# Projecting layer 1's first chunk inside layer 0's tail: a two-layer transformer block on one Trainium2 core

## The chip, the core and the metric

The kernel runs on one core of one Trainium2 chip. The core has five engines with a queue of instructions each: TensorE (PE in the profile, with its weight loads as PEld), VectorE (DVE), ScalarE (ACT), GpSimd (POOL) and SyncE (SP), which here only issues transfers. Work meets in SBUF, in eight PSUM banks of 2 KB per partition, and in DRAM, over 16 DMA engines. The metric is the time of one execution in microseconds (us); before the change three runs gave 1144.49, 1149.3 and 1153.21 us, median 1149.3.

## The reference, cut to what matters

The input x is 2 x 1024 tokens of 256 numbers. Each of two layers computes

```python
xn = _layernorm(x)
x = x + attention(xn) + ffn(xn)
```

Layer 0 has causal attention with 32 heads of 8 over 1024 tokens and a gated feed-forward part with FP8 roundings. Layer 1, whose start the change touches, attends between the 16 heads of one and the same token:

```python
q = apply_rope((x @ wq.T).reshape(b, s, 16, 16), inv_freq)   # k the same way
v = (x @ wv.T).reshape(b, s, 16, 16)
scores = einsum('bshd,bstd->bsht', q, k) / sqrt(16)
attn = einsum('bsht,bstd->bshd', softmax(scores), v)
out = attn.reshape(b, s, 256) @ wo.T
```

Its feed-forward part is `silu(gate) * up` with ternary weights, an RMS norm and a second ternary matrix.

## The kernel before, in words

**Tiles.** The 2048 tokens are 16 tiles of 128 (`xs`), and four tiles make a chunk of 512. `xnT[c]` holds the normalised chunk c with the features on the partitions. Layer 1 takes the chunks in the order 0, 1, 3, 2.

**Layer 0** (`attention0`, from line 802) runs over pairs (b, i): a batch b and a tile of 128 queries i, in an order that ends with (1, 2), (1, 1), (1, 0). The work is laid out by hand in slots. Each pass of `one_slot` (line 1311) emits some units of the row maxima for a later tile (`max_unit`, L1010: matmuls into `ps_s`, three PSUM banks, then a reduction on DVE, L1034), a piece of layer 0's feed-forward part, a piece of a "late" layernorm on every third slot, and whatever `after` has made due. Then `weigh` (L1081) emits the scores of two groups of heads into `ps_t` (four banks), their exponentials on ACT (L1096) and, on the diagonal blocks (j == i), a mask on POOL (L1100). Every second slot `gather` (L1114) adds the products with v of the pair of slots before into `acc` (the eighth bank). `normalise`, `turn_rows` and `output` (L1128 to L1161) follow a finished tile; the last instruction of a tile is the addition of the bias to x on POOL (L1160). PE's order is the order of the code (`manual_schedule`); the order on the other engines is chosen by the compiler's scheduler among what is emitted, with `tc.issue_after` as an extra edge. TAIL = 16: the maxima are spread so that they are all emitted when 16 slots of `weigh` are left. Those slots are the last four of (1, 2), the eight of (1, 1) and the four of (1, 0).

**Layer 1** (`layer1`, from line 408) takes its order from a heap of times written out by hand: `at(delay, f)` (L752) puts f at a time, and the loop at L797 emits in order of these times. For the first chunk (p = 0) they are:

- -5.0, -4.1, -3.2, -2.3: `project(0, i)` (L461) for the four tiles: the product with wq and wk (`pqk`, L467), the rotation by two multiplications on DVE (L475) and an addition on POOL (L482), the product with wv (`pv`, L486), and a copy on ACT (L490). Half a unit of time later `turn` (L493) transposes q and k on PE (`pt`, L498), copies them on ACT (L499), sends all six 128 x 128 squares to a DRAM scratch (`qkv<-all`, L501) and loads from it three pieces of 128 KB: q, k and v by heads, into partitions 32i to 32i + 15 of the slots (`qs`, `ks`, `vs`, L503).
- -4.7 to 2.3 in steps of 1: `ffn_unit(0, hc)` (L666), twelve matmuls `f1gu` (L678) into two banks `ps_gu`, with ACT, DVE and POOL work behind it.
- -1.81 and -0.01: `busy_later` (L766), 7 and 10 matmuls whose results nobody reads (L145).
- -0.4: `project(1, 0)` of the second chunk.
- 0.0: `scores(0, 0)` (L516): `sq` (L522) reads the q and k slots of all four tiles; DVE reduces (L530), the maxima go to DRAM (`mscr<-m`, L532) and come back as a row of the q slot (`qs<-mscr`, L535); then `shifted` (L551) computes the scores again (`sk`, L557) and ACT takes the exponential.

Before all of these, `load_same(0)` (L442) puts eight constant pieces (four of 72 KB from 9 rows, four of 64 KB from 8 rows) into the slots, and POOL fills the v slot with ones (L433). Behind the last load of the first chunk, SP issues `load_same(1)` and the load of `wo` (L508 to L510). The slots take over SBUF from layer 0, so the first of these loads waits for layer 0's last addition on POOL.

The line numbers are those of the kernel before. Three functions carry the change: `two_layers`, `layer1` and `attention0`.

## Time and profile before

| what | us |
|---|---|
| three runs | 1144.49, 1149.3, 1153.21 (median 1149.3) |
| the profiled execution's own time | 1146.81 |
| its span, first to last instruction | 1144.6 |
| PE, DVE, ACT, POOL busy | 1006.4, 761.1, 608.3, 399.9 |
| last reduction of the maxima, start | 733.4 |
| layer 0's last addition on POOL, end | 774.2 |
| first `pqk` of layer 1, start | 772.5 |

The profile is one execution of the program. The page gives totals; the trace behind it answers by engine and by time, counted in us from the start of the span. The chain of waits follows the work back from its last instruction: a line has a start, a length and what ran there, and a line "DMA a<-b" is the time in which the chain waited for that transfer. In a table of stretches, (x n) is the number of instructions, PEclk the share of its full clock that TensorE was granted, and DMA the mean share of the 16 DMA engines in use, added up over their packets, so that it can pass 1.

### The profile page before, as it was taken

Reading aid. Unit: us, or ns where it says so; the run is one execution under the profiler, and the core shown is the slowest. Engines: PE = TensorE matmul, PEld = TensorE weight load, DVE = VectorE, ACT = ScalarE, POOL = GpSimd, SP = SyncE. Lnnn points to the kernel's source line nnn. Section 1 sums busy time; section 2 is a strip of 40 time slices with the busy share of each in tenths; the row PEclk is TensorE's granted clock in tenths of the full one; section 3 lists DMA queues with packets and bytes.
Section 4 is the critical chain, followed back from the end, with each engine's and each line's share of the span. In section 5 each row is a group of like instructions: output and inputs, shape, how many; then the busy total and the mean of one; then the engine's idle time right before and its main releaser. Section 6 shows DMA issues by size and latency. Waiting matters only on the chain.

```text
span 1144.6 us, 19966 instructions
## 1 busy us (share of the span) xinstructions
PE 1006.4 (88%) x7676; PEld 484.2 (42%) x7699; DVE 761.1 (66%) x1434; ACT 608.3 (53%) x1097; POOL 399.9 (35%) x440
## 2 busy tenths in 40 slices
PE   5858797897998989998989989988899999899897
PEld 2333331232332323332323333424577677676576
DVE  6567978889687897889886988504554544543521
ACT  3113571674455757678867767853463444434331
POOL 2007224424135121411133254547644535423400
PEclk9758896998899989999999999999899999999989
DMA  5332101101101000100000100006621241343100
GB/s 177 114 104 78 58 1 41 21 21 35 57 7 42 15 28 10 29 18 7 22 15 14 28 15 17 5 1 105 82 48 38 55 83 34 80 75 52 39 20 20
DMA packets 63888, 49.04 MB, mean 43 GB/s; under 512 B 20905, under 2 KB 57257, under 8 KB 63657
## 3 DMA queue, kind: packets, MB, share of 16 engines
q1 hardware_dynamic: 58592, 39.05, 15.2%
q0 software_dynamic: 4112, 8.26, 3.0%
q8 instruction: 60, 0.98, 0.4%
q10 hardware_dynamic: 1088, 0.46, 0.1%
q14 instruction: 36, 0.29, 0.1%
HBM read 34.12 MB, written 15.20 MB: 43 GB/s over the span
## 4 chain that ended last, share of the span: by engine, by line
PE 51%; DVE 27%; DMA 8%; ACT 7%; POOL 3%; issue 3%; SPq 2%; DVEq 0%; ACTq 0%; POOLq 0%
DVE mx L1034 14%; PE acc L1116 8%; PE s L1086 7%; PE sk L557 4%; PE f1gu L678 4%; PE f1o L717 3%; PE m L1022 3%; PE pqk L467 3%; PE sq L522 3%; DMA qscr<-ptq 2%; PE gu L301 2%; DMA qs<-mscr 2%; ACT p L1096 2%; PE m L994 1%; SPq L946 1%
## 5 line engine op out<-in xcount | busy, mean ns | idle before, releaser
L1034 DVE TENSOR_REDUCE mx<-m 128x1 f32<-128x512 f32 (+3 forms) x608 | 373.0, 653 | 100.5 <-PE m L1022 53.8
L1096 ACT ACTIVATE p<-s 128x512 f32<-128x512 f32 x576 | 307.7, 606 | 123.0 <-PE s L1086 119.0
L1116 PE MATMUL acc<-p,v 128*9 128x512 f32 x1152 | 170.1, 610 | 1.8 <-ACT p L1096 1.2
L1100 POOL TENSOR_SCALAR_AFFINE_SELECT p<-p 128x512 f32<-128x512 f32 x128 | 82.9, 672 | 152.5 <-ACT p L1096 152.3
L1022 PE MATMUL m<-k,qmain 64*128 64x512 bf16 (+3 forms) x384 | 95.5, 358 | 44.4 <-DVE mx L1034 34.5
L1022 PE MATMUL m<-kmain,qmain 64*128 64x512 bf16 (+3 forms) x384 | 81.7, 330 | 21.8 <-DVE mx L1034 20.0
L1022 PEld LDWEIGHTS <-qmain 64*128 64x128 bf16 x768 | 50.5, 99 | 81.3 <-issue 52.1
L994 PEld LDWEIGHTS <-ident_h 64*128 64x128 bf16 x832 | 45.7, 97 | 82.6 <-issue 59.7
L994 PE MATMUL m<-mask_q,ident_h 64*128 64x128 bf16 (+3 forms) x832 | 73.9, 221 | 1.9 <-DVE mx L1034 1.7
L1086 PE MATMUL s<-qmain,k 64*128 64x512 bf16 x288 | 65.8, 394 | 6.3 <-DVE att L1139 2.7
L1086 PE MATMUL s<-qmain,kmain 64*128 64x512 bf16 x288 | 65.3, 385 | 6.7 <-ACT p L1096 4.2
L1086 PE MATMUL s<-qlast,k 35*128 35x512 bf16 x288 | 62.8, 391 | 0.0
L1086 PE MATMUL s<-qlast,klast 35*128 35x512 bf16 x288 | 61.5, 381 | 0.0
L1086 PEld LDWEIGHTS <-k 64*128 64x128 bf16 (+1 forms) x576 | 21.0, 95 | 93.0 <-issue 84.5
L678 PEld LDWEIGHTS <-wgu_bf 128*128 128x128 bf16 x384 | 38.3, 101 | 41.5 <-issue 5.0
L557 PE MATMUL sk<-qs,ks 25*128 25x128 f32 x512 | 48.3, 423 | 8.1 <-DMA qs<-mscr 7.9
L687 DVE SCALAR_TENSOR_TENSOR h<-h,f1gu 128x512 f32<-128x512 f32 x32 | 21.9, 686 | 48.8 <-ACT h L686 48.8
L565 ACT ACTIVATE p<-sk 128x2048 f32<-128x2048 f32 x16 | 30.0, 1877 | 44.3 <-PE sk L557 44.3
L692 POOL TENSOR_TENSOR sq<-h 128x512 f32<-128x512 f32 x28 | 29.1, 1039 | 67.2 <-DVE h L688 65.8
L1159 POOL TENSOR_TENSOR x<-x,aos 128x256 f32<-128x256 f32 x16 | 12.6, 789 | 112.7 <-ACT aos L1158 112.7
L530 DVE TENSOR_REDUCE m<-sq 128x16 f32<-128x2048 f32 x16 | 36.6, 2286 | 20.9 <-PE sq L522 19.3
L154 POOL TENSOR_TENSOR hp<-hrest,hp 128x512 bf16<-128x512 f32 x32 | 37.0, 1157 | 31.5 <-ACT hp L153 31.4
(288 smaller groups left out, 1799.0 us busy)
## 6 DMA issues: line engine op xcount, KB each, us to landing
qmain<-qscr SPq DMA_DIRECT2D x64, 96.0 KB
qkv<-all SPq DMA_DIRECT2D x16, 384.0 KB
qscr<-ptq POOLq DMA_DIRECT2D x6, 384.0 KB, 4.1
x<-in_x SPq DMA_DIRECT2D x16, 128.0 KB
qmain<-qscr SPq DMA_DIRECT2D x32, 64.0 KB
qs<-qkv SPq DMA_DIRECT2D x16, 128.0 KB
ks<-qkv SPq DMA_DIRECT2D x16, 128.0 KB
vs<-qkv SPq DMA_DIRECT2D x16, 128.0 KB
```

The lines of the kernel that those rows point to most:

```text
L154: engines[1].tensor_tensor(parts[2], r, parts[1], ALU.subtract)
L467: nc.tensor.matmul(pqk, x[k], wqk[:, k, :], start=(k == 0), stop=(k == 1))
L530: last(nc.vector.tensor_reduce(m, ps, AX.X, ALU.max, negate=True))
L557: nc.tensor.matmul(ps[:, s, r, :], columns(k, slice(S * s, S * s + HD + 9), 4 * b + r), columns(q, slice(S * s, S * s + HD + 9), 4 * b + r ...
L678: nc.tensor.matmul(ps[g], wgu_bf[:, k, g * HID + hc * P : g * HID + (hc + 1) * P], x_parts[n][m][:, k, :], start=(k == 0 and m == 0), stop ...
L994: nc.tensor.matmul(out[e][:, :, lo:], ident_h[rows, t, :], rhs.to_broadcast([HALF, out[e].shape[1], P - lo]), start=start and t == 0, stop ...
L1022: nc.tensor.matmul(sc[e][:, s * width : (s + 1) * width], qst[b, i][0][rows, p, :], kst[b][0][rows, lo // 512, p // 4, 0:width], start=not ...
L1034: reduced = nc.vector.tensor_reduce(mx[b, i][:, part, e, pairs[0] : pairs[0] + n], sc[e][:, : n * width].rearrange("p (s k) -> p s k", s=n ...
L1086: nc.tensor.matmul(sc[e], kst[b][n][rows, j // 4, u, j % 4 * P : (j % 4 + 1) * P], qst[b, i][n][rows, 4 * u : 4 * u + 4, :], start=n == 0, ...
L1096: nc.scalar.activation(p, sc[e], AF.Exp, scale=scale)
L1100: nc.gpsimd.affine_select(out=by_head, in_=by_head, compare_op=ALU.is_ge, fill=0.0, base=0, pattern=[[0, 4], [1, P]], channel_multiplier=-1,)
L1116: nc.tensor.matmul(acc[32 * s : 32 * s + HD0 + 1, :], vst[b][:, j, 4 * G + s, :], ps[s], start=(j == 0), stop=(j == i),)
```

## The change

Three things go out of layer 1: the four calls of `project` for the first chunk, the `turn` that each of them puts into the heap, and the two `busy_later` entries at -1.81 and -0.01. In their place the heap gets, at -5.0, four calls of `to_slots`, which is the old end of `turn`: the twelve loads from the DRAM scratch (and, behind the last, `load_same(1)` and `wo`, as before).

The work itself goes into layer 0. `first_projections` is a generator of eight steps: `rows(0)`, `rows(1)`, `turned(0)`, `rows(2)`, `turned(1)`, `rows(3)`, `turned(2)`, `turned(3)`. `one_slot` takes one step on every even slot once all maxima are emitted; what is left is emitted behind the last `gather`. `rows(i)` does what `project` did, `turned(i)` what `turn` did up to the transfer to the scratch, with these differences: the PSUM tiles are those of `ps_s`; both copies out of PSUM are on DVE instead of ACT; the tile that goes to the scratch takes a buffer of the tag "parts", of which there are two; `qk` has two buffers and `qk2` one; DVE's instructions are put behind the last reduction of the maxima. The four scratches are tensors of their own and stay. The program's scratch for the descriptors of POOL's transfers is set to 4096.

```diff
--- before.py
+++ after.py
@@ -50,6 +50,8 @@
 def two_layers(ctx: ExitStack, tc: tile.TileContext, a: dict, out: bass.AP):
     nc = tc.nc
     cp = ctx.enter_context(tc.tile_pool(name="const", bufs=1))
+    first_qkv = []
+    dp = ctx.enter_context(tc.tile_pool(name="first", bufs=4, space=bass.MemoryType.DRAM))
     layer0 = ExitStack()
     zp = layer0.enter_context(tc.tile_pool(name="layer0", bufs=1))
 
@@ -499,6 +501,9 @@
                 last(nc.scalar.copy(all_t[:, 0:4], pt))
                 scr = dram.tile([6, P, P], F32, tag="qkv", name=f"qkv{nm}")
                 nc.sync.dma_start(out=scr.rearrange("a p t -> p a t"), in_=all_t)
+                to_slots(c, i, scr)
+
+            def to_slots(c, i, scr):
                 for n, to in enumerate(slots[turn_of[c] % 2]):
                     last_sent[0] = nc.sync.dma_start(
                         out=to[S * i : S * i + HD],
@@ -763,14 +768,14 @@
 
             counter = itertools.count()
 
-            for t, n in ((-1.81, 7), (-0.01, 10)):
-                busy_later(t, ps_s, n)
-
             for t, n in ((29.49, 5), (29.99, 8), (32.9, 4), (33.36, 4)):
                 busy_later(t, ps_gu, n)
             for p, c in enumerate(chunks):
                 for i in range(4):
-                    at(8.0 * (p - 1) + 2.0 * i - 0.4 if p else 0.9 * i - 5.0, lambda c=c, i=i: project(c, i))
+                    if p:
+                        at(8.0 * (p - 1) + 2.0 * i - 0.4, lambda c=c, i=i: project(c, i))
+                    else:
+                        at(-5.0, lambda c=c, i=i: to_slots(c, i, first_qkv[i]))
                 for b in range(4):
                     at(8.0 * p + 2.0 * b, lambda c=c, b=b: scores(c, b))
 
@@ -1160,6 +1165,53 @@
                 nc.gpsimd.tensor_tensor(x_i, x_i, bo_bc, ALU.add)
                 add_done(8 * b + i)
 
+
+            def first_projections():
+                cs, sc = tables
+                shape = [P, 32, 2, 8]
+                made = {}
+
+                def rows(i):
+                    x = [xnT[0][:, k, i * P : (i + 1) * P] for k in range(2)]
+                    pqk = ps_s.tile([P, 512], F32, tag="s", name=f"fpqk{i}")
+                    for k in range(2):
+                        nc.tensor.matmul(pqk, x[k], wqk1[:, k, :], start=(k == 0), stop=(k == 1))
+                    pairs = pqk.rearrange("p (h f e) -> p h f e", f=8, e=2)
+                    qk = pool.tile(shape, F32, tag="fqk", name=f"fqk{i}", bufs=2)
+                    qk2 = pool.tile(shape, F32, tag="fqk2", name=f"fqk2_{i}", bufs=1)
+                    for to, e, tab in ((qk, 0, cs), (qk2, 1, sc)):
+                        nc.vector.tensor_tensor(
+                            to,
+                            pairs[:, :, None, :, e].to_broadcast(shape),
+                            tab[:, None, :, i, :].to_broadcast(shape),
+                            ALU.mult,
+                        )
+                    nc.gpsimd.tensor_tensor(qk, qk, qk2, ALU.add)
+                    pv = ps_s.tile([P, 2, P], F32, tag="s", name=f"fpv{i}")
+                    for u in range(2):
+                        for k in range(2):
+                            nc.tensor.matmul(
+                                pv[:, u, :], wv1[:, k, u * P : (u + 1) * P], x[k], start=(k == 0), stop=(k == 1)
+                            )
+                    all_t = pool.tile([P, 6, P], F32, tag="parts", name=f"fall{i}")
+                    nc.vector.tensor_copy(all_t[:, 4:6], pv)
+                    made[i] = qk, all_t
+
+                def turned(i):
+                    qk, all_t = made[i]
+                    pt = ps_s.tile([P, 4, P], F32, tag="s", name=f"fpt{i}")
+                    flat = qk.rearrange("p h e f -> p (h e f)")
+                    for u in range(4):
+                        nc.tensor.transpose(pt[:, u, :], flat[:, u * P : (u + 1) * P], ident)
+                    nc.vector.tensor_copy(all_t[:, 0:4], pt)
+                    scr = dp.tile([6, P, P], F32, tag="qkv0", name=f"qkv0_{i}")
+                    nc.sync.dma_start(out=scr.rearrange("a p t -> p a t"), in_=all_t)
+                    first_qkv.append(scr)
+
+                for step, i in ((0, 0), (0, 1), (1, 0), (0, 2), (1, 1), (0, 3), (1, 2), (1, 3)):
+                    with tc.issue_after(reduced.ins):
+                        (turned if step else rows)(i)
+                    yield
 
             def rest_of(pieces):
                 for _ in pieces:
@@ -1281,6 +1333,7 @@
                 if next(late[0], self_end) is self_end:
                     late.pop(0)
 
+            projections = first_projections()
             acc = ps_acc.tile([P, 512], F32, tag="acc", name="acc0")
             nc.vector.memset(acc, 0.0)
             pieces = itertools.chain(conversions, ffn0(pool, ps_t, weights, add_done))
@@ -1324,6 +1377,8 @@
                 if late and slot % 3 == 0:
                     with tc.issue_after(reduced.ins):
                         next_late()
+                if at == len(maxima) and slot % 2 == 0:
+                    next(projections, None)
                 pairs_left -= weights
                 tick()
 
@@ -1343,6 +1398,7 @@
                         waiting = (b, i, G, j, group)
                         group = []
             gather(*waiting)
+            rest_of(projections)
             rest_of(pieces)
             while later:
                 tick()
@@ -1441,7 +1497,7 @@
     import concourse.bacc as _bacc
     from concourse.bass_utils import run_bass_kernel_spmd as _run
 
-    nc = _bacc.Bacc("TRN2", target_bir_lowering=False, num_devices=1)
+    nc = _bacc.Bacc("TRN2", target_bir_lowering=False, num_devices=1, dynamic_dma_scratch_size=4096)
     arrays, aps = {}, {}
     for name, v in _arrays(inputs).items():
         v = _np.ascontiguousarray(v)
```

## The prediction

> **What bounds the kernel now.** I read the table of stretches first, for the two places that the change touches. The stretches are layer 0's last 16 slots with the end of layer 0, layer 1 up to its first `sq`, and from there to the end of the second chunk's first projection.
>
> ```profile
> 734.00:772.50 38.50, 35.03 (x200) 10.60 (x198) 4.70 (x18) 24.72 (x50) 16.56 (x27) 1.00 0.01 3
> 772.50:808.20 35.70, 31.89 (x151) 17.65 (x154) 18.89 (x33) 12.77 (x24) 26.92 (x25) 1.00 0.79 106
> 808.20:830.30 22.10, 17.36 (x110) 11.45 (x112) 9.11 (x15) 10.17 (x14) 11.46 (x10) 0.77 0.51 71
> ```
>
> After the time and the length come PE, PEld, DVE, ACT and POOL busy, PEclk, DMA share, GB/s. In the tail PE looks full, DVE is nearly empty and DMA is idle; in layer 1's first 36 us the DMA engines are full; behind that PE's clock falls. Is PE really full in the tail? Its timeline says no:
>
> ```profile
> 740.89 1.04 PE L1116 MATMUL acc<-p,v 128*9 128x512 f32 x8
> ...
> 742.84 2.69 PE L1116 MATMUL acc<-p,v 128*9 128x512 f32 x8
> ...
> 749.36 2.69 PE L1116 MATMUL acc<-p,v 128*9 128x512 f32 x8
> ...
> 757.55 1.53 PE L1116 MATMUL acc<-p,v 128*9 128x512 f32 x8
> ...
> 760.95 1.98 PE L1116 MATMUL acc<-p,v 128*9 128x512 f32 x8
> ```
>
> One `gather` takes 1.04 us where its inputs are there; the rest of the longer ones (1.65, 1.65, 0.49, 0.94) is waiting for POOL's masks. With short gaps elsewhere (0.24 at 740.1, 0.31 at 746.5, 0.43 at 752.9, 0.31 at 760.1) PE waits 6.0 us between 735 and 763. Then the chain of waits across the start of layer 1:
>
> ```profile
> 783.58 0.44 PE pt L498 x4
> 784.02 1.72 PE pqk L467 x4
> 785.73 0.89 PE pv L486 x8
> ...
> 795.85 1.27 POOL qk L482
> ...
> 798.47 3.31 DMA qkv<-all
> ...
> 802.19 6.01 DMA ks<-qkv
> 808.20 2.40 PE sq L522 x31
> 810.63 2.30 DVE m L530
> 812.95 6.22 DMA mscr<-m
> 819.23 2.12 DMA qs<-mscr
> 821.48 3.96 PE sk L557 x31
> 825.44 3.71 PE pqk L467 x4
> ```
>
> Here nothing waits for PE as such: `sq` starts when the k of the fourth tile has landed, `sk` when the maxima are back. The last two lines take twice their usual time. The finer stretches say why, and give the transfers' rates:
>
> ```profile
> 776.00:778.00 2.00, 2.00 (x12) 1.04 (x11) 0.69 (x1) 0.60 (x1) 1.29 (x2) 1.00 0.70 74
> 792.00:794.00 2.00, 1.77 (x10) 0.68 (x8) 0.18 (x1) 0.37 (x1) 1.78 (x2) 1.00 1.24 101
> 794.00:796.00 2.00, 0.00 (x0) 0.00 (x0) 1.71 (x3) 0.62 (x1) 0.15 (x1) 1.00 0.82 178
> 824.00:826.00 2.00, 2.00 (x23) 1.65 (x20) 0.00 (x0) 0.52 (x1) 0.00 (x0) 0.50 1.10 98
> ```
>
> At 776 only the constant pieces of `load_same` run: 74 GB/s. At 792 only loads of q, k, v: 101 GB/s at a share of 1.24, so that is their limit. An idle PE of 3.4 us (793.8 to 797.2) left the clock at 1.00; one of 4.7 us (816.8 to 821.5) brought 0.50 until about 829.
>
> **What the change costs in the tail.** `rows` is 1.72 + 0.89 = 2.61 us of PE, `turned` 0.44 (the chain's rows above): 4 x 3.05 = 12.2 us, in PE's fixed order, one step in every second slot, thus one between each pair's second `weigh` and its `gather`. What of PE's waits they fill: the four `rows` come first, second, fourth and sixth, the `turned` third, fifth, seventh and eighth. The four long waits get a `turned` each: 0.44 x 4 = 1.8 of them. The gaps of 0.24, 0.31 and 0.43 fall to `rows`: 1.0. Together 2.7 (rounded down), left 9.5. The ends are all 6.0 filled (6.2) and nothing filled with POOL's four additions (1.27 each) always ahead of the masks: 12.2 + 5.1 = 17.3. Normally an addition is through before the masks: the DVE products end some 0.5 us after `pv`, and the exponentials that the masks need come over 1.5 us after that `weigh`. I take half a microsecond for them: **+10.0**.
>
> DVE gets per tile two products (0.69, 0.68), and two copies, for which ACT's rows stand in (0.37, 0.59): 9.3 us beside 4.7 busy in 38.5; hidden by that. Queued behind them on DVE are only `z` and `att`; a late one holds a `ps_t` bank. SP gets four transfers to the scratch (3.31 us to land in the chain, 6.0 at 779 beside `load_same`); the DMA share is 0.01, and SP's last loads for layer 0 are issued by 742.4, so nothing waits. `rows(2)` and `rows(3)` need a buffer of "parts" that a transfer must have read: it is issued some 1.5 us behind its `turned`, and the next `rows` copies a pair of slots later (3.5 us as now, plus 2.6); landed in time at 3.3, at 6.0 some 1 us late, on DVE alone. Taken at 0. The smaller descriptor scratch touches POOL's own transfers: six stand close together at 5 to 9 us, landing in up to 8.8 us; the next thing that POOL does is at 32.5. Later ones are over 6 us apart and land in 4 to 6. Taken at 0, at most a few us early on.
>
> **What layer 1 gains.** I count in the clock of before, from the same 774.2 at which the slots come free (the 10.0 is added at the end). Out go 12.2 us of projections, 17 idle matmuls (1.5 + 2.2 us) and the 3.4 us wait for POOL's addition. What stays before `sq`: five `f1gu` units at 2.55 us, held to about 2.9 by the two banks, and `project(1, 0)` with 2.6: PE is ready at 772.5 + 14.5 + 2.6 = 789.6. Now the transfers bound. `load_same(0)`: 0.557 MB at 74 GB/s, 7.5 us, to 782. Its share of 0.70 at that rate is about 1.24 x 9/16, so I read it as filling some 9 of the 16 engines and count the loads behind it in the same queue. Twelve loads of 131 KB at 102 GB/s take 1.28 us each: the eleventh (last k) lands at 782 + 14.1 = 796.2, the twelfth at 797.5. `sq` starts at 797, against 808.2. From the twelfth load to `sk` it took 821.5 - 809.5 = 12.0 us (the twelfth then ended 1.3 behind the `ks` that landed at 808.2), under the same queue of `load_same(1)` and `wo`; so `sk` starts at **809.5 against 821.5: 12.0 us**.
>
> PE idles from 789.6 to 797, more than the 4.7 that halved the clock, and no idle matmuls are left there. At half clock until some 7.5 us after work resumes (821.5 to 829 now), `sq` (4.0 instead of 2.1) and 1.75 us worth of the 6.3 us of filling work run to 804.5, and the other 4.5 to 809: PE just gets to `sk` without a gap, with the clock back. Then `sk`, `pqk` and `pv` take 2.1, 1.9 and 0.9 instead of 3.96, 3.71 and 1.19: **4.0 us** more. Sum 16.0. Bounds: if the loads run beside `load_same` instead of behind it, all is 4 us earlier (`sk` at 805.5, full clock, 20.0); if the clock stays low over `sk`, 12.0.
>
> From the Trainium skill, TensorE: Matmul & The Clock Gate, rules for authors: PE gaps over about 3 us between bursts bring the half clock back, so idle time should be filled. That rule speaks against taking the idle matmuls out. This trace kept full clock through 3.4 us and lost it at 4.7. By the rule alone the slow stretch before `sq` would be charged, about half of 7.5 us, and the sum would be 3.7 us worse; by the rows the slowed work waits for transfers anyway.
>
> **Sum.** +10.0 - 16.0 = -6.0 against the profiled execution's 1146.8 (1144.6 of span and 2.2 around it): 1140.8, rounded to **1141**. That execution lies 2.5 us under the median of the three runs. The likeliest case alone spans 1146.8 + (7 - 18) to 1146.8 + (13 - 14): 1136 to 1146.
>
> **The rivals.**
> - *Loads beside `load_same`* (the trace's 0.70 leaves seven engines free): 20.0 gained, tail at 6.2 to 10: -10 to -13.8, 1133 to 1137. Against it: each load needs its share of the busy engines too. Chance 0.24.
> - *The gain dies in the transfers*: `sq` is earlier, but a second idle stretch before `sk` keeps the low clock: 12.0 gained against 10 to 12: -2 to 0, 1145 to 1147. For it: the mscr transfer waits behind `load_same(1)` today. Chance 0.2.
> - *Slower: the ring of two "parts" buffers.* If a scratch transfer lands 6.0 us or more behind an issue that comes late, DVE stands still in `rows(2)` and `rows(3)`, `att` behind it, and PE waits for its bank. Price up to 6.0 each, 12 for the two: +6, 1153. It decides where the wait reaches 3 us at each place. Against it: DMA share 0.01 there. Chance 0.16.
> - *The change does nothing* (steps emitted behind the last `gather`): PE does the 12.2 serially there, less the 3 us idle at 766 to 772; 9 against 16, nearly the forecast. Not counted apart.
>
> The forecast has 0.4. A measurement here can tell about 1% (11.5 us) from no change. Below 1137.8 lie the first rival, mostly, and a corner of the forecast: 0.25. Above 1160.8 only a corner of the slower rival: 0.08. Within 1%: 0.67. The range 1131 to 1156 takes in the ends 1133 and 1153 and 2 to 3 us for the spread of the runs.
>
> **What would show it.** Layer 0's last POOL addition ends near 784 (774.2 + 10); the first `sq` starts near 807, `sk` near 819.5 in 2.1 us; the low clock lies before and in `sq`, not in `sk`; `pv` of `project(1, 1)` ends near 824 to 825 instead of 830.3. I am wrong if the tail grows by over 16, if DVE waits for a transfer in the tail, or if `sq` waits for POOL or PE and not for `ks`.

## The result, and the profile after

| | before | after |
|---|---|---|
| runs, side by side on one chip | 13 | 13 |
| median, us | 1147.07 | 1154.21 |
| lowest to highest, us | 1143.59 to 1153.21 | 1151.63 to 1159.6 |
| the profiled execution, us | 1146.81 | 1157.42 |
| its span, us | 1144.6 | 1155.7 |

The ratio of after to before is 1.0066, with a 95% interval of 1.005 to 1.0081: 0.7% slower. That is inside the range on record and inside "within 1%", but 13 us above the predicted 1141 and on the other side of no change. The profiled execution of after is 3.2 us above its median, that of before 0.3 us under its own, so the two traces differ by more (11.1 us of span) than the medians (7.1).

I cut both traces at the same instructions: at the last turn of the last late layernorm (the eighth of its `lnt` matmuls on PE, just as the maxima end), and at layer 1's first matmul.

| part of the span, us | before | after | difference | forecast |
|---|---|---|---|---|
| start to the last late layernorm | 734.1 | 742.8 | +8.6 | 0 |
| tail: from there to layer 1's first matmul | 38.3 | 47.9 | +9.5 | +10.0 |
| layer 1 | 372.1 | 365.1 | -7.0 | -16.0 |

(The differences are taken before rounding.) So the tail came as forecast, layer 1 gave back less than half, and something was lost in layer 0 where nothing of the change seems to lie. The stretches of after that answer to the three shown of before (columns: from and to, length, PE, PEld, DVE, ACT, POOL busy, PEclk, DMA share, GB/s):

```profile
742.80:790.60 47.80, 45.35 (x262) 18.36 (x260) 13.76 (x33) 25.66 (x50) 21.23 (x31) 1.00 0.11 35
790.60:826.60 36.00, 25.92 (x130) 13.77 (x130) 19.37 (x29) 12.12 (x21) 25.94 (x24) 0.86 0.85 86
826.60:848.70 22.10, 19.56 (x157) 12.95 (x154) 11.41 (x19) 14.83 (x24) 14.39 (x13) 0.92 0.29 56
```

The tail's stretch is 9.3 us longer, PE is busy 10.3 us more in it, and DVE 9.1: the moved work. In the first 36 us of layer 1 PE is now busy 25.9 instead of 31.9, so it waits, and its clock falls there. PE's timeline in the tail of after:

```profile
746.29 1.05 PE L1193 MATMUL fpv<-xnT,k 128*128 128x128 f32 x8
749.27 1.05 PE L1121 MATMUL acc<-p,v 128*9 128x512 f32 x8
...
755.70 0.66 PE L1205 MATMUL fpt<-ident,fqk 128*128 128x128 f32 x4
756.83 2.06 PE L1121 MATMUL acc<-p,v 128*9 128x512 f32 x8
...
779.38 1.69 PE L1121 MATMUL acc<-p,v 128*9 128x512 f32 x8
```

The `gather` behind a group of `rows` now takes 1.05 us: its masks are there. Behind a `turned` it still waits (2.06, 1.69, where 1.05 is the work): the waits are filled in part, as the forecast had it. The chain of waits of after across the start of layer 1:

```profile
791.62 0.73 POOL x L1165
...
792.40 1.80 POOL vs L435
...
797.80 9.32 DMA vs<-qkv
...
807.14 11.26 DMA ks<-qkv
...
818.53 2.08 PE sq L527 x25
...
820.63 2.30 DVE m L535
...
822.95 5.40 DMA mscr<-m
...
828.41 2.14 DMA qs<-mscr
...
830.69 3.95 PE sk L562 x32
834.64 3.08 PE pqk L469 x4
837.73 0.89 PE pv L488 x8
```

The projections and POOL's addition of q and k are gone from the chain; transfers stand there instead, two of them 9 and 11 us long, and `sk` and `pqk` are as slow as before or nearly.

### The profile page after: what moved, and what is told of

The parts are those of the page before. It is cut to its first block, busy times and chain, and to the rows that moved or that the text cites. A ratio compares the mean times of both kernels' runs of the same rounds, so it can differ in the third digit from the quotient of the medians.

```text
span 1155.7 us, 19948 instructions
## 1 busy us (share of the span) xinstructions
PE 1007.9 (87%) x7682; PEld 483.1 (42%) x7682; DVE 769.6 (67%) x1442; ACT 605.8 (52%) x1089; POOL 400.3 (35%) x440
## 4 chain that ended last, share of the span: by engine, by line
PE 52%; DVE 25%; DMA 8%; ACT 6%; POOL 3%; issue 3%; SPq 2%; DVEq 0%; ACTq 0%; POOLq 0%
DVE mx L1039 13%; PE acc L1121 8%; PE s L1091 7%; PE sk L562 4%; PE f1gu L683 4%; PE m L1027 3%; PE f1o L722 3%; PE sq L527 2%; DMA qscr<-ptq 2%; PE pqk L469 2%; DMA qs<-mscr 2%; PE gu L303 2%; ACT p L1101 2%; PE m L999 1%; SPq L951 1%
## 5 line engine op out<-in xcount | busy, mean ns | idle before, releaser
L1027 PE MATMUL m<-k,qmain 64*128 64x512 bf16 (+3 forms) x384 | 93.7, 359 | 49.9 <-DVE mx L1039 39.5
L683 PEld LDWEIGHTS <-wgu_bf 128*128 128x128 bf16 x384 | 38.5, 101 | 47.3 <-issue 11.0
L535 DVE TENSOR_REDUCE m<-sq 128x16 f32<-128x2048 f32 x16 | 36.6, 2287 | 25.9 <-PE sq L527 24.3
L683 PE MATMUL f1gu<-k,wgu_bf 128*128 128x512 bf16 x192 | 45.0, 385 | 3.8 <-DVE h L692 3.3
```

What stands on the lines that cost most here:

```text
L535: last(nc.vector.tensor_reduce(m, ps, AX.X, ALU.max, negate=True))
L683: nc.tensor.matmul(ps[g], wgu_bf[:, k, g * HID + hc * P : g * HID + (hc + 1) * P], x_parts[n][m][:, k, :], start=(k == 0 and m == 0), stop ...
L1027: nc.tensor.matmul(sc[e][:, s * width : (s + 1) * width], qst[b, i][0][rows, p, :], kst[b][0][rows, lo // 512, p // 4, 0:width], start=not ...
```

## The experiments

Eighteen kernels ran, each beside the kernel before. The table has every ratio to before, and four lengths of its trace in us, cut as above; "first max" and "first exp" run from layer 1's first matmul to the first reduction `m` and the first exponential.

| kernel | ratio (95%) | to the tail | tail | first max | first exp | layer 1 |
|---|---|---|---|---|---|---|
| before | 1 | 734.1 | 38.3 | 38.1 | 53.0 | 372.1 |
| after | 1.0066 (1.005 to 1.0081) | 742.8 | 47.9 | 30.0 | 44.1 | 365.1 |
| e1_small_scratch | 1.0031 (1.0016 to 1.0047) | 738.3 | 38.4 | 39.5 | 53.1 | 374.1 |
| e2_full_scratch | 1.0010 (0.9995 to 1.0024) | 736.1 | 47.9 | 30.0 | 44.1 | 365.1 |
| e3_no_projection | 0.9984 (0.9969 to 0.9999) | 735.0 | 38.4 | 28.8 | 44.1 | 365.0 |
| e4_tail_alone | 1.0092 (1.0062 to 1.0123) | 734.0 | 47.9 | 39.5 | 53.2 | 374.4 |
| e5_same_addresses | 1.0035 (1.002 to 1.005) | 739.2 | 38.3 | 39.5 | 53.1 | 370.3 |
| e6_same_on_act | 1.0018 (1.0001 to 1.0036) | 731.8 | 47.8 | 31.6 | 44.4 | 362.5 |
| e7_v_last | 1.0016 (1.0001 to 1.0031) | 731.3 | 47.8 | 25.0 | 43.6 | 364.7 |
| e8_second_slots_later | 0.9989 (0.9971 to 1.0007) | 732.1 | 47.9 | 28.8 | 40.0 | 358.3 |
| e9_both | 0.9959 (0.994 to 0.9978) | 733.9 | 47.9 | 25.0 | 36.5 | 354.4 |
| e10_before_deferred | 0.9980 (0.9959 to 1.0001) | 733.7 | 38.4 | 39.5 | 50.6 | 370.3 |
| e11_busy_back | 1.0013 (0.9999 to 1.0027) | 733.1 | 47.9 | 28.7 | 43.8 | 361.8 |
| e12_one_issue_moved | 1.0022 (1.0003 to 1.0041) | 734.7 | 38.4 | 39.5 | 53.0 | 370.9 |
| e13_after_issue_moved | 1.0035 (1.0018 to 1.0051) | 737.0 | 47.9 | 28.9 | 43.9 | 364.4 |
| e14_issue_moved_alone | 1.0018 (1.0003 to 1.0034) | 738.1 | 38.3 | 39.5 | 53.1 | 370.8 |
| e15_full_one_copy | 1.0009 (0.9988 to 1.003) | 733.7 | 38.4 | 39.6 | 53.7 | 370.3 |
| e16_full_two_copies | 1.0005 (0.999 to 1.0019) | 731.5 | 38.4 | 39.6 | 53.8 | 370.6 |
| e17_small_one_copy | 1.0050 (1.0027 to 1.0073) | 737.7 | 38.4 | 38.2 | 53.4 | 371.7 |
| e18_full_copy_behind | 1.0036 (1.002 to 1.0052) | 736.5 | 38.4 | 39.5 | 53.6 | 370.4 |

Read the trace columns with care: one execution each. Where layer 1 is that of before, its length lies between 370.3 and 374.4, and the part up to the tail between 731 and 738 without the long product found below. The tail repeats within 0.1 us and the two "first" columns within about 1.5. Layer 1 has a median of 370.8 us over the ten traces that have it as before, and of 365.0 over the four that have it as in after (after, e2, e3, e13): a gain of 5.8 rather than the 7.0 of the one pair. Nor is the profiled execution always a typical one: that of e2 was 3.2 us above the median of its runs, those of e3, e8 and e9 were 2.8 to 4.3 below.

### The parts of the change, one by one

**e1_small_scratch**: the kernel before with the smaller descriptor scratch alone.

```diff
-    nc = _bacc.Bacc("TRN2", target_bir_lowering=False, num_devices=1)
+    nc = _bacc.Bacc("TRN2", target_bir_lowering=False, num_devices=1, dynamic_dma_scratch_size=4096)
```

> The kernel before with the one number changed: the scratch for the descriptors of POOL's transfers is 4096. In the profiles the changed kernel is already 8.6 us late at the last late layernorm (733.3 against 741.9), before any added instruction, with the same order of instructions on every engine. Theory A (the smaller scratch causes that): 5 to 8 us slower than before, ratio 1.004 to 1.007, and the lateness appears between 100 and 180 us. Rival B (chance of the execution: phase of the clock): ratio 0.998 to 1.002.

Measured 1.0031: the scratch alone costs 0.31%, 3.6 us of 1145, less than the 5 to 8 expected.

**e2_full_scratch**: the change without the scratch; `fqk` and `fqk2` take SBUF that is free by then.

```diff
-                    qk = pool.tile(shape, F32, tag="fqk", name=f"fqk{i}", bufs=2)
-                    qk2 = pool.tile(shape, F32, tag="fqk2", name=f"fqk2_{i}", bufs=1)
+                    qk = pool.tile(shape, F32, tag=f"y{i % 2}", name=f"fqk{i}", bufs=1)
+                    qk2 = pool.tile([P, 2, *shape[1:]], F32, tag="fs", name=f"fqk2_{i}", bufs=1)[:, 0]
...
-    nc = _bacc.Bacc("TRN2", target_bir_lowering=False, num_devices=1, dynamic_dma_scratch_size=4096)
+    nc = _bacc.Bacc("TRN2", target_bir_lowering=False, num_devices=1)
```

> The changed kernel with the scratch at its default size; the room comes from buffers that layer 0 is done with (qk in the two y buffers, qk2 in fs). Theory A (the scratch): 5 to 8 us less than the changed kernel, 1147 to 1149, ratio to before 1.000 to 1.003. Rival B (chance): as the changed kernel, ratio 1.005 to 1.008.

Measured 1.0010, with tail and layer 1 as in after to a tenth of a us. The move by itself is about neutral: its interval takes in no change.

**e3_no_projection**: e2, whose tail sends one constant tile four times instead of projecting; it leaves out the first chunk's q, k and v.

```diff
-                for step, i in ((0, 0), (0, 1), (1, 0), (0, 2), (1, 1), (0, 3), (1, 2), (1, 3)):
-                    with tc.issue_after(reduced.ins):
-                        (turned if step else rows)(i)
+                all_t = pool.tile([P, 6, P], F32, tag="parts", name="fall")
+                with tc.issue_after(reduced.ins):
+                    nc.vector.memset(all_t, 0.25)
...
```

> As the full-scratch version, but the tail sends a constant tile four times in place of projecting: it leaves out the first chunk's q, k and v. It shows layer 1's gain without the tail's cost. From the trace of the changed kernel layer 1 gained 7.0 us against before, so 1140, ratio 0.994. The prediction's 16 us would give 1131, ratio 0.986.

**e4_tail_alone**: e2's tail, while layer 1 projects its first chunk again as before.

```diff
+                    at(8.0 * (p - 1) + 2.0 * i - 0.4 if p else 0.9 * i - 5.0, lambda c=c, i=i: project(c, i))
```

> The full-scratch version with layer 1 as before the change, so that the first chunk is projected twice (the tail's copy is not used): the tail's cost alone. From the traces 9.5 us (39.2 to 48.7 from the last late layernorm to layer 1), so 1156.6, ratio 1.008. If PE's waits took up the work, 6 us or less, ratio under 1.0055.

The two halves apart: the tail costs 9.5 us in e4's trace, and 0.92% (10.5 us) by its six runs. Without the projections (e3) the trace has the tail back at 38.4 and layer 1 as in after, and its profiled execution took 1140.4; but that was the shortest of its runs, as e2's was the longest of its own, and the medians, 1143.2 and 1147.6, lie only 4.4 us apart. By the medians, then, the tail costs 10.5 us beside the layer 1 of before and 4.4 beside the new one, and layer 1 gains 8.2 us with the tail (e2 against e4) and 2.2 without it (e3 against before). Some 5 us of e3 I can't explain.

### What the small scratch does

**e5_same_addresses**: the scratch lies in SBUF and moves every tile. Here a pad of 12288 bytes per partition takes its place, so that the addresses are those of before.

```diff
+    pad = ctx.enter_context(tc.tile_pool(name="pad", bufs=1))
+    hole = pad.tile([P, 3072], F32, tag="hole", name="hole")
+    nc.vector.memset(hole[0:1, 0:1], 0.0)
```

> The kernel before with the descriptor scratch at 4096, and an unused tile of 12288 bytes per partition in front, so that every tile lies where it lay before. In the run with the small scratch alone one instruction is longer each time, without a wait: DVE's product fw<-fw,fs takes 1032 ns instead of 794, 16 of them, 3.8 us, all on the engine that bounds layer 0. Theory (the moved addresses): 794 ns again, ratio 0.9985 to 1.0015. Rival (the smaller ring): ratio 1.0015 to 1.005, and 1032 ns or later landings of POOL's transfers.

Measured 1.0035: not the addresses. In the traces of e1, e5 and after one and the same DVE instruction stands out, the feed-forward product `fw<-fw,fs` at 177 to 182 us: the mean of 1032 ns came from this one of 16, and the median is 0.68 us in all. The timelines of DVE and POOL around it, first before, then after (start, length, engine, line):

```profile
172.67 1.06 POOL L919 DMA_DIRECT2D qscr<-ptq  x1 [0.30 <-POOL ptq L839]
172.85 1.11 DVE L349 SCALAR_TENSOR_TENSOR tmg<-tsg,twg 128x512 bf16<-128x512 bf16 x1
...
176.79 1.15 POOL L352 TENSOR_TENSOR tmg<-tmg,tsg 128x512 bf16<-128x512 bf16 x1
177.32 1.17 DVE L318 TENSOR_TENSOR fw<-fw,fs 128x1024 bf16<-128x1024 bf16 x1
177.89 1.09 POOL L1100 TENSOR_SCALAR_AFFINE_SELECT p<-p 128x512 f32<-128x512 f32 x1
```

```profile
177.72 1.06 POOL L924 DMA_DIRECT2D qscr<-ptq  x1 [0.46 <-POOL ptq L844]
177.73 0.68 DVE L351 SCALAR_TENSOR_TENSOR tmg<-tsg,twg 128x512 bf16<-128x512 bf16 x1
...
181.62 1.14 POOL L354 TENSOR_TENSOR tmg<-tmg,tsg 128x512 bf16<-128x512 bf16 x1
181.76 4.96 DVE L320 TENSOR_TENSOR fw<-fw,fs 128x1024 bf16<-128x1024 bf16 x1
182.72 0.62 POOL L1105 TENSOR_SCALAR_AFFINE_SELECT p<-p 128x512 f32<-128x512 f32 x1
183.32 1.14 POOL L355 TENSOR_TENSOR tmg<-tmg,twg 128x512 bf16<-128x512 bf16 x1
184.42 0.62 POOL L1105 TENSOR_SCALAR_AFFINE_SELECT p<-p 128x512 f32<-128x512 f32 x1
185.03 1.14 POOL L356 TENSOR_TENSOR wgu_bf<-tmg,twg 128x512 bf16<-128x512 bf16 x1
```

In before the product waits for the rest of one POOL instruction, gets in, and it is then POOL's mask that is long (1.09 instead of 0.62). In after POOL runs five instructions at their usual lengths without a gap, 181.62 to 186.17, and the product ends 0.55 us behind the last of them. DVE sets layer 0's pace there, so the 3.8 us pass through. Further up these two timelines part in one place: POOL's issue of `qscr<-ptq` begins 0.46 us behind the addition ahead of it instead of 0.30, in every run with the small scratch that leaves this issue on POOL. (With the small scratch five of POOL's six issues of this kind begin 0.42 to 0.64 us behind, in before all six 0.30.) In before it thereby begins ahead of DVE's `tmg` product, which takes 1.11; in after the two begin together, `tmg` takes 0.68, and everything behind meets at another instant.

That leaves two causes: the small ring holds DVE, or the 0.16 us shifts POOL against DVE. Seven kernels go at this.

**e12_one_issue_moved** (small scratch), **e14_issue_moved_alone** (full scratch) and **e13_after_issue_moved** (the kernel after) put this one transfer on SP's queue.

```diff
-                        nc.gpsimd.dma_start(
+                        (nc.sync if (b, c, e) == (1, 1, 0) else nc.gpsimd).dma_start(
```

> The kernel before with the small scratch (as e1), and one POOL transfer, the one issued at about 174.6 us just ahead of the 4.96 us product on DVE, put on SP's queue. If the long product comes from the small ring filling or wrapping, counted over POOL's transfers, it moves to a product beside the next POOL transfer (at about 183 or 206 us), still one of about 5 us, and the total stays at e1's (1.003). Rival (it comes from that transfer's own descriptors): no product is longer than 1.2 us there or later, except the 3 us one that the kernel before has too, and the ratio falls to 0.999 to 1.001. Third: the product at 178 stays long, so that POOL's issue has nothing to do with it.

> The kernel after, with its small scratch, and only the one POOL transfer of about 174 us put on SP's queue. Theory: the long DVE product beside that issue is what the small scratch costs; it falls from 4.96 to about 1.2 to 1.6 us, layer 0 up to the tail takes 731 to 737 us (after 742.8), the tail and layer 1 stay as they are (47.9 and 365.1), and the ratio falls from 1.0066 to the one of the kernel with the full scratch, 1.001 to 1.003. Rival: the small scratch costs elsewhere too; the product becomes short but the ratio stays at 1.004 or above.

> Control: the kernel before with its full scratch and the same transfer on SP's queue. If the move itself costs nothing, the ratio is 0.999 to 1.001; then what the move left in the small scratch's run (1.0022) is a cost of the scratch that no long product shows. If the move costs 1 to 2 us by itself, the ratio is 1.001 to 1.002, and the small scratch's cost was all in that product.

In all three the product takes 1.55 us, with either scratch, and it doesn't reappear at a later POOL transfer, so the ring's filling up is out. (POOL then has its masks behind it, and follows its `tmg` with an instruction that uses the result and starts 0.08 us late; there the product gets in, though it comes 0.15 us behind the start of `tmg`.) e12's time did not fall as clearly as its trace (1.0022): moving the issue costs 1.0018 by itself (e14), and the two differ by 0.04%, far inside their intervals. In the kernel after the move takes 0.31% off, 1.0066 to 1.0035, which lies between the 1.001 to 1.003 expected and the rival's 1.004; of the 0.25% that e13 is above e2, e14's 0.18% can be the price of moving the issue. e13's trace is back at 737.0 up to the tail.

**e15_full_one_copy**, **e16_full_two_copies**, **e17_small_one_copy**: a copy of one number (two in e16) on POOL, meant to shift the issue.

```diff
+                                    made = nc.gpsimd.tensor_copy(small[:, t : t + 1], parts[0:1, 0, t : t + 1])
+                                held.enter_context(tc.issue_after(made.ins))
```

> The kernel before with its full scratch, and one copy of a single number on POOL ahead of the transfer issued at about 173 us. In all runs with the small scratch POOL's issue begins 0.46 us behind the addition ahead of it, with the full scratch 0.30; the trace then shows POOL's five instructions behind it without a gap and DVE's product, which reads two tiles of SBUF, waiting for all five. Theory (only the instant at which POOL's train meets DVE's product decides; the scratch just moves the issue by 0.16 us): a small shift of POOL brings the product of 4.9 to 5.0 us in the full scratch too, ratio 1.002 to 1.004. If the shift is too long or too short the product stays near 1.2 to 1.6; with this run and the next one shift each is tried. Rival (the smaller ring itself blocks DVE): the product stays at 1.2 to 1.6 us, ratio 0.999 to 1.001.

> As the run with one copy, with two copies of a single number, a longer shift. Theory: 4.9 to 5.0 us in at least one of the two. Rival: 1.2 to 1.6 us in both.

> The small scratch with the one copy ahead of the same transfer. Theory: the train meets the product at another instant again, and the product may get in early (1.2 to 1.6 us, ratio 0.999 to 1.001) with the ring as small as before; if it stays at 4.96, both instants lie in the stretch in which DVE loses. Rival (the ring itself): 4.96 us, ratio 1.003.

They shifted nothing and tell nothing: the copy read a third of the tile that was ready early, ran in POOL's wait for ACT, and the issue stayed at 0.30 and 0.46 behind the addition; the product took 1.17, 1.17 and 4.96.

**e18_full_copy_behind** lets the copy read what the addition writes:

```diff
-                                    made = nc.gpsimd.tensor_copy(small[:, t : t + 1], parts[0:1, 0, t : t + 1])
+                                    made = nc.gpsimd.tensor_copy(small[:, t : t + 1], parts[0:1, 2, t : t + 1])
```

> The kernel before with its full scratch and a copy of one number on POOL between the last addition and the transfer, so that the issue can't begin before the copy is through (in the three runs before it the copy slipped in ahead of the addition, where POOL waited anyway, and shifted nothing). Theory (the instant decides): the issue begins 0.1 to 0.4 us later against DVE; if it begins behind the start of DVE's product tmg, as with the small scratch, that product takes 0.68 instead of 1.11, and the product fw,fs falls into POOL's train and takes 4.9 to 5.0 us with the full scratch; ratio 1.002 to 1.004. Rival (the ring itself): the issue is shifted as said, and fw,fs stays at 1.2 to 1.6, ratio 0.999 to 1.001. If the copy itself holds DVE off, tmg stays near 1.1 and the run tells nothing.

DVE and POOL in e18, whose scratch is the full one:

```profile
172.58 0.53 POOL L923 COPY small<-ptq 1x1 bf16<-1x1 bf16 x1
172.99 1.11 DVE L349 SCALAR_TENSOR_TENSOR tmg<-tsg,twg 128x512 bf16<-128x512 bf16 x1
173.05 1.07 POOL L925 DMA_DIRECT2D qscr<-ptq  x1
...
176.89 1.14 POOL L352 TENSOR_TENSOR tmg<-tmg,tsg 128x512 bf16<-128x512 bf16 x1
177.03 4.96 DVE L318 TENSOR_TENSOR fw<-fw,fs 128x1024 bf16<-128x1024 bf16 x1
```

Counted from the start of the addition ahead of it, the issue begins 0.23 us later (1.69 instead of 1.46 in e15), the product meets POOL's `tmg` 0.14 us behind its start as in after, and takes 4.96 us with the full scratch; the runs say 1.0036. One thing came otherwise than expected: `tmg` on DVE stayed at 1.11 and the product behind it took 0.68 in its stead. The expectation had said that with `tmg` near 1.1 the run would tell nothing. It does tell: the product met POOL's train as in after, and took 4.96 with the ring at its full size. So the long product is shown to be a matter of timing and not of the ring: 0.2 us on POOL decide whether a DVE product waits for one POOL instruction or for five.

From the Trainium skill, SBUF — State Buffer, "Who interferes with whom": a DVE instruction with two inputs in SBUF contends with a GpSimd instruction that reads SBUF, and the order of issue decides who blocks. The traces agree (`fw,fs` are two such inputs), and add that DVE did not get in between POOL's instructions when they followed each other at once: 4.4 us over five of them.

### What bounds the start of layer 1

All are e2 with one edit, except e9, which has two, and e10.

**e6_same_on_act**: the constant rows of `load_same(0)` from ACT's queue, so that they don't stand ahead of the loads on SP.

```diff
+                queue = nc.sync if n else nc.scalar
...
```

> The full-scratch version with load_same(0) issued from ACT's queue, so that SP's loads of q, k, v need not wait for the landing of those eight transfers. Theory T1 (nine of the sixteen DMA engines have 22.9 us of bytes, the constant pieces and the loads): the first reduction of layer 1 starts as in the full-scratch version, 30.0 us after layer 1's first matmul, within 1 us. Rival T2 (SP keeps 8 transfers in flight and each load waits for one to land): 3 to 4 us earlier, 26 to 27 us, and 0 to 4 us less in all.

First max 31.6 instead of 30.0: no earlier, and 0.6 us outside what I had expected. The queue is not the limit; that the engines' bytes are is my reading, which e7 supports. (From the Trainium skill, DMA: Bandwidth & Descriptors, "Issuing engines are not separate DMA queues": transfers from several engines share the 16 DMA engines. That the first max came no earlier, at 31.6, agrees.)

**e7_v_last**: q and k of all four tiles loaded ahead of v.

```diff
-                        at(-5.0, lambda c=c, i=i: to_slots(c, i, first_qkv[i]))
+                        at(-5.0, lambda c=c, i=i: to_slots(c, i, first_qkv[i], range(2)))
+                        at(-4.9, lambda c=c, i=i: to_slots(c, i, first_qkv[i], [2]))
```

> The full-scratch version with the eight loads of q and k ahead of the four of v. sq needs q and k alone: it starts three loads (3.8 us) earlier, so the first reduction 26 us after layer 1's first matmul instead of 30.0. sk waits for the maxima, whose transfer stands behind load_same(1) and wo in either order: if that queue ends it (my reading), sk and the whole move by less than 1 us; if sq's start does, all is 3.8 us less.

The first max is 5.0 us earlier and the first exponential 0.5: the gain is lost again in the maxima's way through memory. In the traces 3.8 us of it go on SP's queue, where `mscr<-m` stands behind the second slots' rows and `wo` and waits for its turn, and 0.7 in the transfer, 6.2 us instead of 5.5.

**e8_second_slots_later**: `load_same(1)` and `wo` issued behind the first maxima's way back.

```diff
-                if c == chunks[0] and i == 3:
-                    with tc.issue_after(last_sent[0].ins):
-                        load_same(1)
...
+                if c == chunks[0] and b == 0:
+                    last_sent[0] = sent
+                    second_slots()
```

> The full-scratch version with load_same(1) and wo issued behind the first maxima's return to the q slot. The maxima's transfer then goes alone: 1.4 us as where the queue is empty (1047.6 in the trace of before) instead of 5.4, so the first exponential of layer 1 starts 40 us after layer 1's first matmul instead of 44.1, and 3 to 4 us less in all, ratio 0.997 to 0.999 to before. If the whole does not move, the saved time is given back at the second chunk's slots.

First exponential 4.1 us earlier, layer 1 6.8 us shorter in the trace; by the runs 0.9989 against e2's 1.0010, about 2.4 us.

**e9_both** has both edits.

> e2 with both changes of the order of layer 1's loads: q and k before v, and the second slots' rows and wo only after the first maxima. Theory (layer 1's front is bound by bytes on the DMA engines ahead of what the scores wait for): sq's first maximum as in the run with v last (25.0 us after layer 1's first matmul instead of 30.0) and the maxima's round trip as short as in the run with the second slots later (11 us from there to the first exponential instead of 14), so the first exponential at 36 us (e2 44.1), layer 1 355 to 358 us (e2 365.1), total 1139 to 1143, ratio 0.994 to 0.998. Rival (the two overlap, because something else, POOL's five FFN units or the v loads now beside the maxima, is the next bound): first exponential at 39 to 40, layer 1 as with the second slots later alone (358.3), ratio 0.999.

SP's issues around the first maxima, in after and then in e9:

```profile
819.77 0.27 SPq L442 DMA_DIRECT2D qs<-in_same  x1
821.02 0.39 SPq L515 DMA_DIRECT2D wo<-in_wo  x1
822.95 0.36 SPq L537 DMA_DIRECT2D mscr<-m  x1
...
828.41 2.49 SPq L540 DMA_DIRECT2D qs<-mscr  x4
```

```profile
809.11 0.35 SPq L539 DMA_DIRECT2D mscr<-m  x1
...
810.59 2.49 SPq L542 DMA_DIRECT2D qs<-mscr  x4
813.12 0.51 SPq L441 DMA_DIRECT2D ks<-in_same  x1
```

From the issue of the 8 KB of maxima to that of their way back it takes 5.46 us behind the second slots' rows and `wo`, and 1.48 ahead of them. The two gains add up: first exponential at 36.5, layer 1 354.4, and 0.9959 (1141.1 us): the only complete kernel of the study that is clearly faster than before, with its interval ending at 0.9978.

**e10_before_deferred**: the kernel before, nothing moved, with e8's edit.

> The kernel before, nothing moved, with only the second slots' rows and wo after the first maxima. If the maxima's way through memory was held by those transfers in the kernel before too, the first exponential comes 3 to 5 us earlier (53.0 us after layer 1's first matmul becomes 48 to 50), layer 1 366 to 369 us (372.1), ratio 0.995 to 0.998: then the order of the loads pays as well without the move as with it. Rival: in the kernel before the loads of the projections take so long that load_same(1) has drained by the first maximum, and nothing changes (53, ratio 1.000).

First exponential 50.6 instead of 53.0, a little less than expected, and 0.998. Whether the order of the loads pays without the move too is not shown: the interval takes in 1, and layer 1, at 370.3, is no shorter than in e5 and e15, which leave it as it was. With the move and v last it does pay.

**e11_busy_back**: the idle matmuls put back ahead of the first scores.

```diff
+            for t, n in ((-1.81, 7), (-0.01, 10)):
+                busy_later(t, ps_s, n)
```

> e2 with the two groups of 7 and 10 idle matmuls ahead of the first scores put back, which the change took out. They run in the wait for the loads. Theory (sk is paced by the landing of the four maxima pieces): sk still takes 3.9 to 4.1 us, the first exponential at 43.5 to 44.5 us, ratio to before 1.000 to 1.002 as e2. Rival (the forecast's term: sk, pqk and pv are slow from the half clock after an idle PE): sk 2.1, pqk 1.9, the first exponential 3 to 4 us earlier, ratio 0.997 to 0.998.

First exponential 43.8, `sk` 4.06: the idle matmuls are worth nothing here. They kept the clock full over `sq`, and it fell in `sk` instead (0.62 and 0.50 granted there), so this run alone does not say what makes `sk` slow. After's own stretches do:

```profile
814.00:816.00 2.00, 0.20 (x1) 0.00 (x0) 0.00 (x0) 0.00 (x0) 1.50 (x2) 0.50 0.65 63
...
830.00:832.00 2.00, 1.31 (x5) 1.15 (x5) 1.86 (x5) 1.21 (x3) 0.70 (x1) 1.00 0.11 3
832.00:834.00 2.00, 2.00 (x27) 1.83 (x27) 0.23 (x1) 0.00 (x0) 1.92 (x3) 0.89 0.95 151
834.00:836.00 2.00, 2.00 (x10) 1.19 (x5) 0.00 (x0) 1.32 (x1) 0.82 (x1) 0.50 0.62 54
```

The half clock came in the wait for `sq`, as forecast, was over by 828, and `sk` began at full clock, which fell again only in its last 1.1 us, and still took 3.95: five matmuls in its first 1.3 us, then 27 in the next two. Each group of four reads all four pieces of the maxima, which SP issues one after the other over 2.49 us. Counted from the first issue of `qs<-mscr` to the end of `sk` it is the same everywhere: 6.2 us in before (819.23 to 825.44, half clock), 6.2 in after (828.41 to 834.64, full for the first 5.1), 6.5 in e9, where `sk` began only when the pieces had landed and took 2.11. A later stretch of before shows it as well, with `sk` at 4.10 us and the clock at 1.00 and 0.98:

```profile
1051.23 4.10 PE L557 MATMUL sk<-qs,ks 25*128 25x128 f32 x32
```

```profile
1051.00:1053.00 2.00, 1.90 (x8) 1.47 (x6) 1.16 (x2) 1.38 (x4) 1.59 (x2) 1.00 0.17 21
1053.00:1055.00 2.00, 2.00 (x28) 1.82 (x27) 0.00 (x0) 0.57 (x1) 2.00 (x2) 0.98 1.14 155
```

Nor does the half clock slow `sk` or `sq` where their inputs are there. A later `sk` of before ran at 0.50 throughout and took 2.12 us, as at full clock in e9 (2.11):

```profile
1089.58 2.12 PE L557 MATMUL sk<-qs,ks 25*128 25x128 f32 x32
```

```profile
1089.50:1091.70 2.20, 2.20 (x34) 1.90 (x33) 0.00 (x0) 1.94 (x3) 0.00 (x0) 0.50 0.00 0
```

The last 26 matmuls of the first `sq` took 2.07 us in after, at 0.50, and 2.05 in e11, at 1.00. `pqk` is another matter: 3.71 us in before at 0.50 (825.44), 1.72 at 1.00 (784.02).

## Why the prediction was wrong, point by point

Two terms of the sum failed. Layer 1's gain was put at 16.0 us and came to 7.0 in the traces; the descriptor scratch was put at 0 and cost 3.6. Without the scratch the move is at 1.0010 (e2), where the forecast stood at 0.995; the scratch then made it clearly slower.

**The tail, +10.0: right.** Measured +9.5 in after, and 9.5 in e4 against e1; by the runs between 4.4 (e2 against e3) and 10.5 (e4). The 12.2 us of PE work fill part of PE's waits, and POOL's last addition ends at 792.4, which is 783.7 when the 8.6 us lost before the tail are taken off (forecast: near 784).

**DVE copies, scratch transfers, the ring of "parts", 0: right.** The tail's length leaves no room for a DVE stall, and e2 with the same steps comes out neutral. The slower rival that I priced at 1153 did not happen, though the time is near its own.

**The descriptor scratch, "taken at 0, at most a few us early on": this step failed.** It measured 3.6 us alone (e1) and 0.31% in after (after against e13). I looked at how long POOL's transfers take to land, which did not change, and not at when their issue starts. A bound "at most a few us" stood in the text and was not carried into the sum. The rest of the 8.6 us I leave open: 4.8 us beyond the long product, of which the medians show less (e1 and e2 add up to 1.0041, after has 1.0066; the intervals just allow for the difference). It goes with the granted clock: up to the tail TensorE stood at half clock for 133 us in after's trace and for 116 in before's, and over the twenty traces this time rises with the length up to the tail less the long product (0.18 us per us, correlation 0.86), which would make 3.1 of the 4.8. Which of the two brings the other is not shown, and e14, with the full scratch, has 133 us as well.

**Layer 1, 12.0 us up to `sk`: mis-sized, 9.0.** From the first issue of `load_same(0)` to the start of `sk` before took 47.3 us (774.22 to 821.48), after takes 38.3 (792.37 to 830.69), and I had 35.3. The order was right (PE ready first, the loads last, `sq` waiting for `ks`), and the rate of a load (1.2 us from issue to issue, forecast 1.28) nearly. What I missed is the end: the constant pieces load only some of the engines, the loads behind them pile up on those, and the last k, issued at 807.14, lands 11.26 us later while the others run dry and the second slots' rows start. In the stretch from 814 the DMA share is 0.65 at 63 GB/s, where it had been 1.25 at 106 from 810 to 812. This reading of the shares is argued; shown is that the queue is not it (e6), and that fewer bytes ahead of `sq` bring it forward (e7, 5.0 us).

**Layer 1, 4.0 us from the clock in `sk`, `pqk` and `pv`: this failed.** They took 3.95, 3.08 and 0.89 against the forecast's 2.1, 1.9 and 0.9, so 0.9 of 4.0 came. In before the half clock and the slow `sk` stood at the same place, and I read one as the cause of the other. `sk` waits for the fourth piece of the maxima at either clock, and with its inputs there it takes 2.12 us at 0.50 too; `sq`, put at 4.0 at half clock and 2.1 at full, took 2.07 at 0.50. `pqk`, which the half clock does slow, then met a second, short stretch of it (0.50 from 834 to 836). The row of the Trainium skill on gaps over about 3 us (TensorE: Matmul & The Clock Gate, "Why this matters for your kernels"; the prediction names the section otherwise) says when the half clock comes back, and not what it costs an instruction.

**The sum.** Of the 16.0 us, 9.9 had come by the end of that `pv` (56.1 us after the first `load_same` in before, 46.3 now). Layer 1 as a whole shows 7.0; the 2.9 between lie in its later chunks, and traces of an unchanged layer 1 differ there by as much (370.3 to 374.4), so I give them no cause. With +9.5 in the tail the move alone was bound to end near zero: e2's 1.0010. Of the rivals, "the gain dies in the transfers" (12.0 gained against 10 to 12, 1145 to 1147) describes the move itself best, but not by its cause, a low clock; the sign came from the scratch.

## What to carry to other kernels

When work is moved out of a stage that ends on transfers, price the order of the queue behind it first: here two edits of the order of the loads, with nothing computed differently, turned a neutral move into 0.4%. A slow stretch that coincides with a low clock is not yet explained by it: find an instance of the same instruction at full clock, and one at half clock with its inputs there, and compare. And a side setting that "only" shifts one engine's issue by 0.2 us must be measured by itself, because instructions that share a port can fall into another order.

## What the runs showed of the hardware

- A DVE product of two SBUF tiles (median 0.68 us) took 4.96 us behind five POOL instructions in direct succession, alike in five traces (4.955 to 4.958), and 1.17 or 1.55 in all others. Why DVE gets in behind POOL's `tmg` when it comes 0.53 us after its start, and not when it comes 0.14 after, stays open; in e12 to e14 it came 0.15 after and got in, where POOL paused for 0.08 us.
- With a descriptor scratch of 4096, five of POOL's six issues of a 384 KB transfer began 0.42 to 0.64 us behind the instruction ahead of them instead of 0.30; the transfers landed as before (4.0 to 6.0 us).
- A transfer of 8 KB to memory and the start of its way back took 1.48 us on idle DMA engines (e9) and 5.46 us behind `wo` and pieces of 64 to 72 KB that occupy few partitions (after).
- At a granted clock of 0.50 a group of 32 `sk` matmuls took 2.12 us and at 1.00 2.11, while `pqk` took 3.71 and 1.72. Why `sk` does not feel the clock stays open.
